# Eight small moves in the written order of a two-block kernel's second block

## The chip, the cores and the metric

The kernel runs on one core of a Trainium2 chip. The metric is the device time of one launch in microseconds (us), the median of three runs. The engines are named as in the profile: PE (TensorE, matmuls and transposes), DVE (VectorE), ACT (ScalarE), POOL (GpSimd), SP (the queue that issues most DMAs).

## The reference, cut to what matters

x is 2 x 1024 tokens of 256 features, all in float32. There are two blocks, each with a residual connection around it.

```
# first block
x = x + soft_moe(attention_with_field(x, cond))      # 16 heads of 16; 64 experts of 32 slots
# second block
h = rotation(x)                                       # a 256 x 256 matrix from quaternions
for l in range(2):                                    # two layers, 8 heads of 64, windows of 128 tokens
    q, k, v = split(shift_token(h) @ wqkv[l])
    q, k = l2norm(q) * q_scale[l], l2norm(k) * k_scale[l]
    q, k = rotary_xpos(q, k)                          # q*cos*scale + rotate_half(q)*sin*scale, k with 1/scale
    h = h + local_attention(q, k, v) @ wo[l]          # each window looks at itself and the one before
    t = shift_token(h)
    t = (t - mean(t)) / sqrt(var(t) + 1e-5) * ln_g[l] + ln_b[l]
    a, g = split(t @ w1[l] + b1[l])                   # 682 + 682 features
    h = h + (a * gelu(g)) @ w2[l] + b2[l]
x = x + h
```

In the soft mixture of experts the output is a product of softmax weights (2048 per token, over all slots) with the experts' outputs. The kernel computes this last product, called the mixing here, partly beside the first windows of the second block.

## The kernel before, in words

**The second block** (from L1060) is one loop over steps s from -2 to 31. There are 32 windows of 128 tokens: window i belongs to layer i // 16, batch i // 8 % 2 and place i % 8. The order of the instructions on PE, DVE, ACT and POOL is the order in which the code issues them; only the order of DMA issues on SP is left to the scheduler. Step s works on several windows at once, in this order:

- project(s+2) (L1115): four matmuls of 128x512 into a PSUM tile pq, for q and k. rotate_parts(s+2) (L1130): ACT copies pq to raw and squares it; DVE multiplies pq with the cosines into t1 (L1143, "the cosine product"); POOL multiplies raw with the sines in two halves into t2 (L1145). Both ACT's copy and DVE's product read the same PSUM banks, and the build orders them one behind the other, as issued.
- scores (L1202): q times k into PSUM. maxima (L1219): four DVE instructions per half of the heads that add the mask, scale and reduce. weights (L1239): four exponentials on ACT per half. turn_e (L1263): transposes of the divided weights of the window before, copied by ACT (first half of the heads) or DVE (second half). mix (L1280): weights times values.
- values and keep_values (L1173): the value projection. turn (L1189): transposes of the rotated q and k. norms(s+2) (L1150): DVE sums the squares (L1154) and makes a first guess z (L1157); POOL refines it in twelve small instructions to zn (L1161 to L1164). rotated(s+2) (L1168): DVE adds t1 and t2 (L1170) and scales the k half with zn (L1171).
- divide (L1254): four divisions per half by the softmax sums, on POOL for the first half, on DVE for the second (L1260).

After every fourth window project_out (L1303) adds the attention's output to the residual into xb (L1314, DVE), and halves (L1324, POOL) adds the two feature halves for the mean of chunks 1 to 6. A chunk is 512 tokens; chunk f runs through forward(s - 7), four steps each: centre(f) makes the mean on PE (L1333), subtracts it on DVE (L1341) and squares on ACT (L1343); normalise(f) makes the variance on PE (L1333), the reciprocal root on ACT by a logarithm and an exponential (L1353, L1354), multiplies on DVE (L1355, hc times rs) and scales on POOL (L1357); gate (L1363) makes one of six pieces of the w1 product; feed (L1394) the w2 product. The first chunk has centre(0) at the end of step 5 and normalise(0) at the end of step 6; its first gates come at the end of step 7.

**The mixing beside it.** In steps -2 to 4, beside(s, point) (L1509) runs one sixteenth of the mixing of the second batch at the points "a", "b" and, in the first two steps, "c" of a step: combine (L902) multiplies a turned piece of the weights with the experts' outputs (at the end of four pieces DVE adds the sum, L920), then turn_w (L883) transposes the next piece (L888) into a two-bank PSUM tile, and ACT (odd pieces, L895) or DVE (even pieces, L897) copies it to xb. READY (L1495) names where the rows of the weights are made: heaviest (the row maximum, DVE), weigh (the exponential, ACT), scale (reciprocal and division by the sum, DVE, L880 and L881). From step 5 on a step is "dense": both halves' scores stand together.

**PSUM.** Two-bank tiles come from two_banks (L1091). There are three: two in the pool ps_b and one in ps_c, called the third. While the mixing runs, the third holds the sums of combine and only the other two rotate. From the first tile behind the last mixing product on, a counter (ring) lets all three rotate, so that each tile takes the place of the one three before it and waits for its readers; the tile with len(ring) % 3 == 1 is the third.

**Tables.** weights2 (L1013) loads the weights of a layer. For "tabs" it issues two DMAs of 512 KB (the cosines and the sines with their scales) and has POOL multiply them with q_scale and k_scale (L1021, four instructions). For the second layer it stands at the end of step 13, behind the second half's divisions.

Of the kernel before, what the change touches and what calls it, by code (L numbers as in the profile page):

```python
# [10 lines left out]
F32 = mybir.dt.float32  # L11
I32 = mybir.dt.int32
AF = mybir.ActivationFunctionType
ALU = mybir.AluOpType
# [3 lines left out]
P = 128  # L18
B = 2
# [11 lines left out]
H1, DH = 8, 64  # L31
# [51 lines left out]
def bcast(ap, axis, n):  # L83

    ap = ap.unsqueeze(axis)
    shape = list(ap.shape)
    shape[axis] = n
    return ap.to_broadcast(shape)
# [3 lines left out]
def tile_kernel(ctx: ExitStack, tc: tile.TileContext, a: dict, out: bass.AP):  # L92
    nc = tc.nc
# [789 lines left out]
    def turn_w(q, jj):  # L883

        pt = wide("pe")
        for j in range(4):
            for i in range(2):
                nc.tensor.transpose(  # L888
                    pt[:, j // 2, (j % 2 * 2 + i) * P : (j % 2 * 2 + i + 1) * P],
                    row(2 * q + i)[:, (4 * jj + j) * P : (4 * jj + j + 1) * P],  # L890
                    ident,
                )
        wTs[q, jj] = xb[:, jj % 2, 1, 1 : 1 + S].rearrange("p (x n) -> p x n", x=2)
        if jj % 2:
            nc.scalar.copy(wTs[q, jj], pt)  # L895
        else:
            nc.vector.tensor_copy(wTs[q, jj], pt)  # L897
        for i in (2 * q + 4, 2 * q + 5):
            if i < T // P:
                fetch(i, jj)  # L900
# [68 lines left out]
    with tc.manual_schedule(  # L969
# [36 lines left out]
        load = {}  # L1006
# [66 lines left out]
    with tc.manual_schedule(  # L1073
# [12 lines left out]
        def third(name):  # L1086
            return ps_c.tile([P, 2, 512], F32, tag="c", name=name)
# [3 lines left out]
        def two_banks(name):  # L1091

            if not mixing:
                ring.append(name)
            return third(name) if len(ring) % 3 == 1 else ps_b.tile([P, 2, 512], F32, tag="b", name=name)

        wide, pair = two_banks, third

# [31 lines left out]
        def rotate_parts(i):  # L1130

            w = i % NWIN
            pq = pqs.pop(i)
            raw = dx0.tile([P, 16, DH], F32, tag="keep", name="raw")
            nc.scalar.copy(raw, pq)  # L1135
            sqs[i] = la.tile([P, 16, DH], F32, tag="t", name="sq", bufs=3)
            nc.scalar.activation(sqs[i], raw, AF.Square)
            t1 = la.tile([P, 16, DH], F32, tag="t", name="t1", bufs=3)
            t2 = la.tile([P, 16, DH], F32, tag="t2", name="t2", bufs=1)
            hf = DH // 2  # L1140
            p4, r4, t14, t24 = (t.rearrange("p (x h) d -> p x h d", x=2) for t in (pq, raw, t1, t2))
            cos, sin = (t[:, :, w, :] for t in load["tabs"])
            nc.vector.tensor_tensor(t14, p4, bcast(cos, 2, H1), ALU.mult)  # L1143
            for lo, hi in ((0, hf), (hf, DH)):
                nc.gpsimd.tensor_tensor(  # L1145
                    t24[:, :, :, lo:hi], r4[:, :, :, hf - lo : DH - lo], bcast(sin[:, :, lo:hi], 2, H1), ALU.mult
                )
            ts[i] = t1, t2
# [167 lines left out]
        def chunk(f):  # L1316

            return f // (B * 2), f // 2 % B, f % 2 * 512
# [28 lines left out]
        def normalise(f):  # L1347
            l, b, t0 = chunk(f)
            hc, sq = hcs[f], hcs.pop((f, "sq"))
            pv = bank("pvar")  # L1350
            sums(f, pv, [sq[:, k, :] for k in range(2)])
            rs = fa["rs"]
            nc.scalar.activation(rs, pv, AF.Ln, bias=eps5)  # L1353
            nc.scalar.activation(rs, rs, AF.Exp, scale=-0.5)  # L1354
            nc.vector.tensor_tensor(hc, hc, bcast(rs, 1, 2), ALU.mult)  # L1355
            for k in range(2):
                nc.gpsimd.tensor_scalar(  # L1357
                    hc[:, k, :], hc[:, k, :], col(f"lg{l}", k), col(f"lb{l}", k), ALU.mult, ALU.add
                )
# [105 lines left out]
        def forward(at):  # L1465

            f, k = divmod(at, 4)
            if at == -2:
                centre(0)
            if at == -1:  # L1470
                normalise(0)
            if not 0 <= f < CHUNKS:
                return
            if k == 0:
                gate(f, 0)
                gate(f, 1)
            if k == 1:
                gate(f, 2)
                gate(f, 3)
            if k == 2:  # L1480
                gate(f, 4)
                if f + 1 < CHUNKS:
                    centre(f + 1)
                gate(f, 5)
            if k == 3:
                if f + 1 < CHUNKS:
                    normalise(f + 1)
                feed(f)


# [7 lines left out]
            (-2, "b"): ((scale, 11),),  # L1498
            (-1, "c"): ((heaviest, 12), (heaviest, 13)),
            (-1, "b"): ((weigh, 12), (weigh, 13)),  # L1500
            (-1, "e"): ((scale, 12), (scale, 13)),
            (0, "c"): ((heaviest, 14),),
            (0, "b"): ((weigh, 14),),
            (1, "c"): ((scale, 14), (heaviest, 15)),
            (1, "b"): ((weigh, 15),),
# [16 lines left out]
        for s in range(-2, WINDOWS):  # L1522
            now, before, nxt, new = (0 <= s + d < WINDOWS for d in (0, -1, 1, 2))

            if new:
                project(s + 2)
                rotate_parts(s + 2)
            ended = 0 <= s - 2 < WINDOWS

            late = s >= WINDOWS - 2
            dense = s > max(PARTS) and not late
            if ended and not dense and not late:
                mix(s - 2, 1)
            if now and dense:
                for hg in range(2):
                    scores(s, hg)
            if ended and dense:
                for hg in range(2):  # L1540
                    if (s - 2, hg) in eTs:
                        mix(s - 2, hg)
            if s == 5:
                rotate(3)
            if now and not dense and not late:
                scores(s, 0)
            beside(s, "a")
            if before:
                turn_e(s - 1, 0)
            if now and not late:  # L1550
                maxima(s, 0)
                weights(s, 0)
            if new:
                values(s + 2)
                keep_values(s + 2)
            beside(s, "c")
            if ended and late:
                for hg in range(2):
                    if (s - 2, hg) in eTs:
                        mix(s - 2, hg)  # L1560
            if now:
                for hg in () if dense else (0, 1) if late else (1,):
                    scores(s, hg)
                for hg in (0, 1) if late else (1,):
                    maxima(s, hg)
                    if hg == 0:
                        weights(s, 0)
            if before and not dense:
                mix(s - 1, 0)
            if nxt:  # L1570
                turn(s + 1)
            if now:
                weights(s, 1)
            if new:
                norms(s + 2)
            beside(s, "b")
            if 0 <= s - 2 < WINDOWS and (s - 2) % 4 == 3:
                project_out((s - 2) // 4)
                if (s - 2) // 4 in halved:
                    halves((s - 2) // 4)  # L1580
            if before:
                turn_e(s - 1, 1)
            if now:
                divide(s, 0)
            if new:
                rotated(s + 2)
            if s == 5:

                f = xp.tile([P, 4 * NS], F32, tag="e", name="f")
                at = 0  # L1590
                for name, k, n in (("u", NF, 512), ("w2", NF, D), ("yo", 2, 512), ("rs", 1, 512), ("sq", 2, 512), ("gl", 2, 512)):
                    fa[name] = f[:, at : at + k * n].rearrange("p (k n) -> p k n", k=k)
                    at += k * n
                fa["rs"] = fa["rs"][:, 0, :]
                fa["hc"] = xin.tile([P, 2, 2, 512], F32, tag="x1", name="hc")
                load["w2"] = fa["w2"]
                load["w1"] = xp.tile([P, NE // 4 * D], F32, tag="y1", name="w1")[:, : 2 * W1N].rearrange(
                    "p (k n) -> p k n", k=2
                )
                weights2(0, "w1", "w2")  # L1600
            forward(s - LAG)
            if now:
                divide(s, 1)
            beside(s, "e")
            if s + 2 == B * NWIN - 1:
                weights2(1, "wqkv", "tabs")
            if s == B * NWIN + 2:
                weights2(1, "wo")
            if s == LAG + 4 * (CHUNKS // 2) - 2:
                weights2(1, "w1")  # L1610
            if s == LAG + 4 * (CHUNKS // 2) - 1:
                weights2(1, "w2")
# [13 lines left out]
        centre(f + 1)  # L1626
        gate(f, 4)
        normalise(f + 1)
        feed(f)
        for n in (0, 1, 2, 3, 5, 4):  # L1630
            gate(f + 1, n)
# [119 lines left out]
```

## Time and profile before

| | |
|---|---|
| median of three runs | 1614.73 us (1613.99 to 1615.87) |
| the profiled execution | 1613.42 us, of it the span 1611.4 us |
| busy, share of the span | PE 98%, DVE 57%, ACT 55%, POOL 33% |
| granted TensorE clock | 1.00 throughout |
| second block (its first projection starts at 846.6): PE busy in 900 to 950, 950 to 1000, 1000 to 1050, 1150 to 1200 | 48.28, 48.69, 47.07, 48.50 of 50 us each |
| PE busy in every other 50 us from 1050 to 1600 | 50.00 of 50 us |
| DVE busy in 1000 to 1050 | 32.77 of 50 us |

A row of the list of waits reads: who waited, "<-" for what, the time in total, how often, the longest. A row of the timeline reads: start and duration in us, engine, line, operation, out<-in, shape, how many were merged; in brackets the idle time before it and what ended that. A matmul in float32 leaves two records. The ends of matmuls are modelled, so that groups on PE overlap by 0.07 or 0.16 us where nothing is waited for.

### The profile page before, as it was taken

How to read it: one execution, taken by the hardware profiler on the slowest of the kernel's cores; microseconds unless marked ns; L12 is line 12 of the kernel's file. 1: busy time of each engine (PE TensorE's matmuls, PEld its weight loads, DVE VectorE, ACT ScalarE, POOL GpSimd, SP SyncE). 2: the span in 40 equal slices, each digit the busy share in tenths (PEclk: the TensorE clock that was granted, in tenths of full speed). 3: DMA queues.
4: the chain of work that ended last, by engine and by line, in shares of the span. 5: the costliest groups of instructions: out<-in, count | busy, mean ns of one | idle time of the engine just before them, and what ended most of it. 6: DMA issues, size and time to landing. Idle time of an engine off the chain costs nothing.

```text
span 1611.4 us, 22677 instructions
## 1 busy us (share of the span) xinstructions
PE 1584.6 (98%) x8672; PEld 805.8 (50%) x8672; DVE 910.6 (57%) x1598; ACT 892.4 (55%) x1662; POOL 538.9 (33%) x830
## 2 busy tenths in 40 slices
PE   8999999999999999999999999999999999999999
PEld 4333333333333444444887666555555555655554
DVE  5768758766773222225455765656576665656532
ACT  2477768777886222226134554666646565666631
POOL 4223323333330100000102345545565555555411
PEclk9999999999999999999999999999999999999999
DMA  5100000010000544455642102000100001000001
GB/s 158 53 14 14 1 15 13 1 21 8 1 1 23 168 142 144 158 166 180 205 123 84 40 1 81 0 1 1 66 1 1 14 1 55 1 1 27 10 18 39
DMA packets 49852, 82.66 MB, mean 51 GB/s; under 512 B 4552, under 2 KB 25200, under 8 KB 49488
## 3 DMA queue, kind: packets, MB, share of 16 engines
q1 hardware_dynamic: 47200, 75.38, 15.4%
q0 software_dynamic: 1584, 5.29, 1.1%
q8 instruction: 68, 1.11, 0.3%
q10 hardware_dynamic: 960, 0.56, 0.1%
q14 instruction: 40, 0.33, 0.1%
HBM read 56.04 MB, written 20.97 MB: 48 GB/s over the span
## 4 chain that ended last, share of the span: by engine, by line
PE 93%; DVE 4%; ACT 1%; issue 1%; DMA 1%; POOL 0%; ACTq 0%; DVEq 0%; POOLq 0%
PE pga L1374 9%; PE sc L329 8%; PE po L347 7%; PE pm L295 7%; PE lg L795 7%; PE sl L821 7%; PE pq L1121 7%; PE cmb L909 5%; PE py L1401 4%; PE pwo L1310 3%; PE po L1290 3%; PE sc L1210 3%; PE pe L1271 3%; PE pv L1177 3%; PE pqk L265 2%; PE py L842 2%
## 5 line engine op out<-in xcount | busy, mean ns | idle before, releaser
L302 DVE TENSOR_REDUCE mx<-pm 128x2 f32<-128x1024 f32 x256 | 302.3, 1219 | 118.1 <-PE pm L295 117.4
L337 ACT ACTIVATE e<-sc 128x512 f32<-128x512 f32 (+1 forms) x500 | 266.1, 612 | 72.3 <-PE pm L295 44.7
L329 PE MATMUL sc<-qs,km 32*128 32x512 f32 x1024 | 254.7, 619 | 0.9 <-DVE qs L317 0.9
L295 PE MATMUL pm<-km,qm 32*128 32x512 f32 x1024 | 246.0, 619 | 2.4 <-ACT xa L432 0.6
L365 POOL TENSOR_TENSOR ob<-ob,part 128x512 f32<-128x512 f32 x101 | 128.3, 1271 | 270.2 <-ACT part L364 270.2
L1374 PE MATMUL pga<-hc,w 128*128 128x512 f32 x320 | 141.8, 593 | 0.0
L1260 POOL TENSOR_SCALAR e<-e,den 128x256 f32<-128x256 f32 (+1 forms) x128 | 130.7, 1034 | 31.4 <-DVE den L1256 31.4
L347 PE MATMUL po<-e,v 128*32 128x512 f32 x1024 | 136.7, 604 | 0.0
L1145 POOL TENSOR_TENSOR t<-raw,tabs 128x512 f32<-128x512 f32 x64 | 81.7, 1296 | 153.6 <-ACT raw L1135 148.3
L329 PEld LDWEIGHTS sc<-qs,km 32*128 32x128 f32 x1024 | 87.6, 183 | 84.5 <-ACT e L337 64.4
L1244 ACT ACTIVATE e<-e,nmx 128x256 f32<-128x256 f32 (+1 forms) x256 | 123.6, 487 | 2.9 <-DVE nmx L1227 2.7
L1121 PE MATMUL pq<-wqo,xa 128*128 128x512 f32 x256 | 115.9, 595 | 1.6 <-DVE xb L897 0.9
L909 PE MATMUL cmb<-xb,y 128*128 128x256 f32 x512 | 116.6, 380 | 0.2 <-ACT xb L895 0.2
L795 PE MATMUL lg<-phi,xa 128*128 128x512 f32 x256 | 115.9, 595 | 0.3 <-ACT xa L432 0.3
L821 PE MATMUL sl<-dsp,xb 128*128 128x512 f32 x256 | 114.9, 592 | 0.0
L295 PEld LDWEIGHTS pm<-km,qm 32*128 32x128 f32 x1024 | 82.8, 183 | 60.0 <-DVE mx L302 31.7
L1227 DVE CUSTOM_DVE_ANT_0 e<-sc,mask,zn 128x256 f32<-128x256 f32 (+1 forms) x256 | 101.9, 460 | 17.4 <-PE sc L1210 17.4
L909 PEld LDWEIGHTS cmb<-xb,y 128*128 128x128 f32 x512 | 94.9, 190 | 16.6 <-issue 3.2
L805 DVE TENSOR_TENSOR l<-lg,keep 128x512 f32<-128x512 f32 x32 | 22.1, 691 | 143.5 <-ACT keep L803 143.5
L1374 PEld LDWEIGHTS pga<-hc,w 128*128 128x128 f32 x320 | 59.0, 190 | 66.6 <-issue 64.5
L1135 ACT COPY raw<-pq 128x1024 f32<-128x1024 f32 x32 | 32.4, 1012 | 107.1 <-PE pq L1121 107.0
L803 ACT COPY keep<-lg 128x512 f32<-128x512 f32 x32 | 18.7, 584 | 125.2 <-issue 107.4
(219 smaller groups left out, 2459.7 us busy)
## 6 DMA issues: line engine op xcount, KB each, us to landing
lgd<-keep SPq DMA_DIRECT2D x64, 256.0 KB, 2.4
w<-in_ffn_W SPq DMA_DIRECT2D x16, 1024.0 KB, 6.9
ebig<-lgd SPq DMA_DIRECT2D x64, 256.0 KB, 3.4
wqo<-in_wqkv SPq DMA_DIRECT2D x2, 1536.0 KB, 7.7
w<-in_w SPq DMA_DIRECT2D x2, 1386.0 KB, 6.1
km<-hk SPq DMA_DIRECT2D x32, 64.0 KB, 2.3
qm<-hq SPq DMA_DIRECT2D x32, 64.0 KB, 2.3
phi<-in_phi SPq DMA_DIRECT2D x1, 2048.0 KB, 7.6
```

Source lines behind the costliest of these rows:

```text
L295: nc.tensor.matmul(pm[:, x, :], qm[u % 2][r, i * P : (i + 1) * P], km[u % 3][r, n * 512 : (n + 1) * 512], start=True, stop=True,)
L302: nc.vector.tensor_reduce(mxs[hu][:, i % 4, 2 * half : 2 * half + 2, n], pm, AX.X, ALU.max)
L329: nc.tensor.matmul(sc[:, x, :] if both else sc[x], km[u % 3][r, j * P : (j + 1) * P], qs[u % 2][r, n * 512 : (n + 1) * 512], start=True, s ...
L337: nc.scalar.activation(part, t, AF.Exp, scale=1.0 / HD0**0.5)
L347: nc.tensor.matmul(po[32 * hh : 32 * hh + 32, :], v[b][:, j, at : at + 32], es[s, hh // 2][:, hh % 2, :], start=True, stop=True,)
L365: nc.gpsimd.tensor_tensor(obs[u, n], obs[u, n], part, ALU.add)
L795: nc.tensor.matmul(lg[:, b, :], xa[:, k, b, 1 + m * P : 1 + (m + 1) * P], phi[:, k, n * 512 : (n + 1) * 512], start=(k == 0), stop=(k == 1),)
L821: nc.tensor.matmul(accs[n][b][:, c, :], xo_tm[:, b * 8 + m, c * P : (c + 1) * P], d[:, b, :], start=(m == 0), stop=(m == 7),)
L909: nc.tensor.matmul(acs[q][:, c, :], y[b][:, 4 * jj + j, c * P : (c + 1) * P], eT[:, j // 2, j % 2 * 256 : (j % 2 + 1) * 256], start=(jj == ...
L1121: nc.tensor.matmul(pq[:, x, :], shifted(xa, k, b, w * WIN, P), load["wqkv"][:, k, x * 512 : (x + 1) * 512], start=(k == 0), stop=(k == 1),)
L1260: engine.tensor_scalar(e[:, x, c, lo:], e[:, x, c, lo:], den[:, x, c : c + 1], None, ALU.mult)
L1374: nc.tensor.matmul(pt[:, x, :], load["w1"][:, k, lo : lo + P], hcs[f][:, k, :], start=(k == 0), stop=(k == 1))
```

## The change

Eight moves, all in the second block or in the mixing beside it; no computation is added or taken away.

- turn_w: for q of 6 and 7 the copies change engines (ACT copies the even pieces, DVE the odd ones).
- two_banks: the third PSUM tile is the third of the rotation (len(ring) % 3 == 0) instead of the first.
- rotate_parts: for window 9 alone DVE's cosine product is issued ahead of ACT's copy of the same tile, so that the copy waits for the product.
- normalise is cut in two: normalise ends with the reciprocal root, normalised has DVE's product and POOL's scaling. For the first chunk normalised(0) stands behind rotate_parts(9) in step 7; for all others both follow each other as before.
- centre(0) moves from the end of step 5 to behind project(8) and rotate_parts(8) in step 6.
- READY: the scale of row 13 moves from point "e" of step -1 to point "c" of step 0.
- In steps 0 to 4 the maxima of the first half stand ahead of point "a" and of the transposes of the window before, instead of behind them.
- The tables of the second layer stand behind norms(15) in step 13, ahead of project_out, the halves and the divisions, and in the code ahead of wqkv. The order of the DMA issues on SP is the same in both kernels (tables, then wqkv).

```diff
         wTs[q, jj] = xb[:, jj % 2, 1, 1 : 1 + S].rearrange("p (x n) -> p x n", x=2)
-        if jj % 2:
+        if jj % 2 != (q > 5):
             nc.scalar.copy(wTs[q, jj], pt)
         else:
             nc.vector.tensor_copy(wTs[q, jj], pt)
...
-            return third(name) if len(ring) % 3 == 1 else ps_b.tile([P, 2, 512], F32, tag="b", name=name)
+            return third(name) if ring and len(ring) % 3 == 0 else ps_b.tile([P, 2, 512], F32, tag="b", name=name)
...
+            sqs[i] = la.tile([P, 16, DH], F32, tag="t", name="sq", bufs=3)
+            t1 = la.tile([P, 16, DH], F32, tag="t", name="t1", bufs=3)
+            cos, sin = (t[:, :, w, :] for t in load["tabs"])
+
+            def cosines():
+                nc.vector.tensor_tensor(
+                    t1.rearrange("p (x h) d -> p x h d", x=2),
+                    pq.rearrange("p (x h) d -> p x h d", x=2),
+                    bcast(cos, 2, H1),
+                    ALU.mult,
+                )
+
+            ahead = i == LAG + 2
+            if ahead:
+                cosines()
             raw = dx0.tile([P, 16, DH], F32, tag="keep", name="raw")
             nc.scalar.copy(raw, pq)
-            sqs[i] = la.tile([P, 16, DH], F32, tag="t", name="sq", bufs=3)
             nc.scalar.activation(sqs[i], raw, AF.Square)
-            t1 = la.tile([P, 16, DH], F32, tag="t", name="t1", bufs=3)
             t2 = la.tile([P, 16, DH], F32, tag="t2", name="t2", bufs=1)
...
-            nc.vector.tensor_tensor(t14, p4, bcast(cos, 2, H1), ALU.mult)
+            if not ahead:
+                cosines()
...
             nc.scalar.activation(rs, pv, AF.Ln, bias=eps5)
             nc.scalar.activation(rs, rs, AF.Exp, scale=-0.5)
+            hcs[f, "rs"] = rs
+
+        def normalised(f):
+            l = chunk(f)[0]
+            hc, rs = hcs[f], hcs.pop((f, "rs"))
             nc.vector.tensor_tensor(hc, hc, bcast(rs, 1, 2), ALU.mult)
...
-            if at == -2:
-                centre(0)
             if at == -1:
                 normalise(0)
...
                 if f + 1 < CHUNKS:
                     normalise(f + 1)
+                    normalised(f + 1)
                 feed(f)
...
-            (-1, "e"): ((scale, 12), (scale, 13)),
-            (0, "c"): ((heaviest, 14),),
+            (-1, "e"): ((scale, 12),),
+            (0, "c"): ((scale, 13), (heaviest, 14)),
...
                 project(s + 2)
                 rotate_parts(s + 2)
+
+            if s == LAG - 1:
+                centre(0)
+            if s == LAG:
+                normalised(0)
...
             if now and not dense and not late:
                 scores(s, 0)
+                maxima(s, 0)
             beside(s, "a")
             if before:
                 turn_e(s - 1, 0)
             if now and not late:
-                maxima(s, 0)
+                if dense:
+                    maxima(s, 0)
                 weights(s, 0)
...
                 norms(s + 2)
+            if s + 2 == B * NWIN - 1:
+                weights2(1, "tabs", "wqkv")
             beside(s, "b")
...
             beside(s, "e")
-            if s + 2 == B * NWIN - 1:
-                weights2(1, "wqkv", "tabs")
```

More of the change, by code (lines that the diff above doesn't have):

```diff
@@ L1133, in rotate_parts @@
             pq = pqs.pop(i)
+            sqs[i] = la.tile([P, 16, DH], F32, tag="t", name="sq", bufs=3)
[11 more added lines that the diff above has]
+                cosines()
             raw = dx0.tile([P, 16, DH], F32, tag="keep", name="raw")
             nc.scalar.copy(raw, pq)
-            sqs[i] = la.tile([P, 16, DH], F32, tag="t", name="sq", bufs=3)
             nc.scalar.activation(sqs[i], raw, AF.Square)
-            t1 = la.tile([P, 16, DH], F32, tag="t", name="t1", bufs=3)
             t2 = la.tile([P, 16, DH], F32, tag="t2", name="t2", bufs=1)
             hf = DH // 2
-            p4, r4, t14, t24 = (t.rearrange("p (x h) d -> p x h d", x=2) for t in (pq, raw, t1, t2))
-            cos, sin = (t[:, :, w, :] for t in load["tabs"])
-            nc.vector.tensor_tensor(t14, p4, bcast(cos, 2, H1), ALU.mult)
+            r4, t24 = (t.rearrange("p (x h) d -> p x h d", x=2) for t in (raw, t2))
+            if not ahead:
+                cosines()
             for lo, hi in ((0, hf), (hf, DH)):
@@ L1628, in tile_kernel @@
         normalise(f + 1)
+        normalised(f + 1)
         feed(f)
```

## The prediction

> **What bounds the kernel now.** I read the page's first two parts first.
>
> ```profile
> span 1611.4 us, 22677 instructions
> ...
> PE 1584.6 (98%) x8672; PEld 805.8 (50%) x8672; DVE 910.6 (57%) x1598; ACT 892.4 (55%) x1662; POOL 538.9 (33%) x830
> ...
> PEclk9999999999999999999999999999999999999999
> ```
>
> TensorE sets the time: 98% busy at the full granted clock, no other engine above 57%. All that reordering can win is its idle time, 26.8 us in all, so next comes the list of PE's own waits.
>
> ```profile
> PE pe L1271 <- DVE t L1143: 4.0, 2, 2.5
> ...
> PE pq L1121 <- DVE xb L897: 0.9, 2, 0.4
> ...
> PE pe L1271 <- DVE xT L920: 0.8, 1, 0.8
> ...
> PE pm L1333 <- DVE xb L1314: 0.4, 1, 0.4
> ...
> PE pe L888 <- DVE t L1143: 0.4, 1, 0.4
> ```
>
> These seven waits (6.6 us of idle) all lie in the second block, and each is at a place that the diff touches. After 1184.97 PE has no wait of 15 ns or more, so what is won before that should reach the end. Third, the timeline around three of them.
>
> ```profile
> 1014.65 1.98 PE L1333 MATMUL pm<-xb,ones_d 128*128 128x512 f32 x4 [0.44 <-DVE xb L1314]
> ...
> 1034.61 0.63 ACT L1354 ACTIVATE f<-f 128x512 f32<-128x512 f32 x1
> ...
> 1035.27 1.30 DVE L1355 TENSOR_TENSOR hc<-hc,f 128x1024 f32<-128x1024 f32 x1 [2.73 <-ACT f L1354]
> ...
> 1036.69 1.89 DVE L1260 TENSOR_SCALAR e<-e,den 128x256 f32<-128x256 f32 x4
> ...
> 1038.50 1.20 DVE L1143 TENSOR_TENSOR t<-pq,tabs 128x1024 f32<-128x1024 f32 x1
> ...
> 1039.85 1.06 PE L1271 MATMUL pe<-ident,e 128*128 128x128 f32 x8 [2.49 <-DVE t L1143]
> ...
> 1179.10 4.69 DVE L1260 TENSOR_SCALAR e<-e,den 128x256 f32<-128x256 f32 x4
> ...
> 1179.80 5.12 POOL L1021 TENSOR_TENSOR tabs<-tabs,rows 128x512 f32<-128x512 f32 x4
> ...
> 1183.71 1.21 DVE L1143 TENSOR_TENSOR t<-pq,tabs 128x1024 f32<-128x1024 f32 x1
> ...
> 1184.97 1.09 PE L1271 MATMUL pe<-ident,e 128*128 128x128 f32 x8 [1.50 <-DVE t L1143]
> ```
>
> The reader is to see two queues of DVE. At 1035 DVE stands for 2.73 us before the chunk's multiplication (L1355), because ACT's reciprocal root is late; four divisions and then the cosine product (L1143) are queued behind it, and PE needs the PSUM tile that this product reads. At 1179 the four divisions take 4.69 us instead of the 1.15 that the same four take at 1153, while POOL multiplies the tables.
>
> **The change, part by part.** Times are on the clock of the trace before; every saving moves what follows. PE starts a group 0.07 or 0.16 us before the modelled end of the group in front, so the end of a wait wins the idle time plus that overlap.
>
> *Scale 13 behind step 0's projection.* One division of a row (L881, 2.29 us at 892.57) leaves the place in front of the cosine product, which would then start when the raw copy ends (892.42) and end at 893.7 instead of 895.99. PE is ready at 895.45: 0.43 + 0.16 = **0.59**. At its new place DVE was idle (3.3 us before 900.40, waiting for a DMA), so it costs nothing; its reader, the transposes at 904, has 6 us to spare. The next PE wait, 0.61 at 914, hangs on POOL's norms (zn at 910.04) and moves along unchanged.
>
> *Copies exchanged, maxima moved ahead of them.* From q = 6 the copy at point "b" goes to ACT, that at "a" to DVE. At "b" of steps 2 and 3 DVE's copy ended at 949.75 and at 971.42, each 0.06 before PE's projection could start. ACT's rows for this copy are 1.01 against DVE's 1.23, ACT is free there (last exponential until 947.09) and its copy can start at 948.53: 0.21 each, **0.42**. The two other "b" copies (904.9, 924.1) had no PE waiting. At "a" DVE's copy would end at 939.72 (transposes end 938.46, plus 1.23) and its first reader of the slot is at 940.98. It must queue behind the maxima, which is why these are issued first: that moves no start, they stand ready at 934.55. Queued behind the copy now: the scale of row 15 (936.17 to about 939.7, needed at 947) and in step 1 that of row 14 and the maximum of row 15, about 0.9 late, with zn then at 926.4 against its use at 929.9.
>
> *Third PSUM tile third.* With three tiles in rotation the phase only matters at the start. The first tile behind the last mixing product took the third buffer and so waited for the sums L920 (991.75); now it takes one whose last readers, the maxima of step 4, ended at 987.2: 0.85 + 0.16 = **1.0**. The third tile, scores of step 5, meets L920 instead, about 3.5 us after it ended. DVE's chain behind (copy 992.93, L1170, L1171, divisions, cosines) starts 1.0 earlier too, as zn (992.33) is ready in time; the projection for the rotation, which started at 999.30 on the heels of these cosines (999.25), moves along.
>
> *First mean behind a projection.* The mean's four matmuls (1.72) no longer stand right behind the sum L1314 (1014.60). PE goes on at 1014.05 with the projection (3.43), then the mean, and the scores start at about 1019.3 instead of 1020.00: **0.70**. On DVE the two subtractions (1.27) go behind the cosines: these come at 1019.6, the subtractions end at 1022.0, and the maxima start at 1021.95 instead of 1022.35. On ACT the square goes behind raw and its square and ends at 1023.1, in time for the copy at 1023.2. The value projection must now wait for the subtractions (PSUM slot): it comes at 1024.05, 2 us later.
>
> *First product behind the cosines.* On the clock shifted by 0.70, the norms' seed z comes at 1026.8 instead of 1027.21 and zn 4.6 after it, as in the trace (1031.81), at about 1031.4; L1171 ends at 1032.1, and the four divisions (1.8) follow at once: 1034.05. The projection ended at 1032.84. Cosines 1034.0 to 1035.2, then raw, which must now wait for them (same banks), to 1036.25. PE reaches its transposes at 1036.6: no wait by a margin of 0.34, **2.49 + 0.07 = 2.56**. The trace has no raw that waits for a product. From one side nothing is lost; from the other, one more collision of POOL's norms with L1170 (an L1161 of 1.24 instead of 0.21) would make all 1.0 later and cost 0.7. I take the margin as worked out; the product of 1.30 then ends at 1036.5, the maxima run from 1036.4 (1039.62 before).
>
> *Tables behind the norms.* Four POOL multiplications (5.12) move from 1179.80 to 1165.74, where POOL stood idle for 4.92 (until 1170.67). The order of SP's queue is not moved: both tables are issued at 1158.74 before the weights, and land after 4.6 (median), about 1164. They end at about 1170.9; the halves' sum (1.09) comes 0.3 later, at 1172.0, PE's mean needs it at 1173.48. The four divisions at 1179.10 then take 1.15, the cosines start with raw's end (1180.70) and PE is not held: 1.50 + 0.07 = **1.57**. POOL's sines also start at 1180.75 instead of 1184.99.
>
> Sum: 0.59 + 0.42 + 1.0 + 0.70 + 2.56 + 1.57 = **6.84 us**. The profiled execution took 1613.42 (span 1611.4 and 2.0 around it), so a profile of the changed kernel would show a span near 1604.6. The median of the three runs is 1.3 above that execution: 1614.73 - 6.84 = **1607.9**.
>
> **Rivals.**
>
> *A. Raw becomes the wait.* The 0.34 margin is a difference of two long chains. For it: DVE is 66% busy in 1000 to 1050, zn is an estimate. Against: PE waits only for what is over the margin. It would leave 0.7, at most 1.5, of the 2.49: 1608.6 to 1609.4.
>
> *B. The first gate waits for the chunk's scaling.* POOL now does the two sines (2.52) before the two scalings (1.76), from raw's end: 1036.29 to 1040.55. The gate comes at 1040.96, its second half at 1041.39: it holds PE only if POOL slips by over 0.84. With both sines as slow as the slowest row (2.26) it would slip by 2.0: 1609.1. In the trace an L1161 of POOL grew from 0.21 to 1.24 beside DVE's L1170 (1029.65). [...]
>
> *C. Another engine takes over the pace.* If DVE's queue, not PE, carried the stretch 890 to 1040, each wait would come back a few instructions on, and only the tables' and half of the cosines' share would last: 1.57 + 1.28, 1611.9, no difference. Against it: every next wait above has a margin.
>
> *D. Slower: POOL's queue stands at the tables.* The multiplications now stand in front of the halves' sum, the divisions and the chunk's square sum, and wait for a DMA. If the second table lands at L, PE's mean is held from L = 1169.8 on (two multiplications 2.56, the halves 1.09). The slowest of the four table loads took 11.1 to land: 1170.6, a wait of 0.8, 1608.7. For a slower kernel PE must lose 10 us, so L at 1180, 20 us after the issue; PE itself would by then wait for the weights behind the tables. Nothing in the trace is near that.
>
> **How the numbers follow.** The forecast 0.62, A 0.14, B 0.06, C 0.12, D as slower 0.03, other places 0.03 slower. What a measurement of this kernel tells from no change is about 0.2%, 3.2 us (the three runs spread over 1.9). Forecast, A and B are faster, 0.82; C is same, 0.12; slower 0.06. Low end: the two PE waits that I leave (0.61 at 914 and 0.66 at 928, for a copy of ACT) could go too with their overlaps, 6.84 + 1.5: 1606.4. High end: A with B, and 1 us for the spread, and part of C: 1611.5. Outside stay most of C, the slower cases and a few in a hundred below.
>
> **What would show it.** Right: in PE's waits the pairs with L897, L920, the first L1314 and both of 2.5 and 1.5 are gone, those with den and xa stay; the product stands behind the cosines; divisions beside POOL's sines at 1.15. Wrong: a PE wait for raw or for POOL's scaling near 1030 to 1036, or for the halves' sum near 1168; PE's idle time unchanged or a new wait after 1180.

## The result, and the profile after

The changed kernel takes 1606.78 us (median of 4 runs, 1606.37 to 1606.99) against 1615.16 us for the kernel before (4 runs, 1613.99 to 1615.87) beside it: a ratio of 0.9952, with a 95% interval of 0.994 to 0.9964. It is faster by 8.4 us, which is more than the 3.2 us that a measurement can tell from no change. In two further comparisons the ratio was 0.9952 (0.9938 to 0.9965; 1606.36 us) and 0.9953 (0.994 to 0.9965; 1607.0 us).

The profiled execution of the changed kernel took 1606.93 us, with a span of 1604.9 (before: 1613.42 and 1611.4). The page's first two parts:

```profile
span 1604.9 us, 22678 instructions
...
PE 1584.1 (99%) x8672; PEld 806.0 (50%) x8672; DVE 905.7 (56%) x1598; ACT 893.0 (56%) x1662; POOL 539.4 (34%) x830
...
PEclk9999999999999999999999999999999999999999
```

PE's busy time is the same within 0.5 us (1584.6 before), so all the gain is idle time of PE. These are PE's waits in the second block, from 840 us to the end; the columns are the total, how often, and the longest:

```profile
PE pe L888 <- DVE ebig L881: 0.8, 1, 0.8
PE pq L1122 <- ACT xa L937: 0.7, 1, 0.7
PE pe L1286 <- DVE nmx L1242: 0.6, 1, 0.6
PE pq L1122 <- ACT xb L896: 0.5, 2, 0.2
PE cmb L910 <- ACT xb L896: 0.2, 1, 0.2
```

What is left is less than 1 us each. The pairs with the cosine product (2.5, 1.5 and 0.4), with the sum L920 and with xb L1314 are gone. The two waits for DVE's copies are halved and now hang on ACT's. PE's idle time from 840 us on (gaps of 15 ns and more) falls from 8.95 to 2.83 us.

The timeline around the first chunk's product, in the changed kernel:

```profile
1030.56 1.68 DVE L1275 TENSOR_SCALAR e<-e,den 128x256 f32<-128x256 f32 x4
...
1032.15 1.21 DVE L1140 TENSOR_TENSOR t<-pq,tabs 128x1024 f32<-128x1024 f32 x1
1032.19 0.63 ACT L1369 ACTIVATE f<-f 128x512 f32<-128x512 f32 x1
...
1033.28 1.26 DVE L1375 TENSOR_TENSOR hc<-hc,f 128x1024 f32<-128x1024 f32 x1
1033.45 1.02 ACT L1152 COPY raw<-pq 128x1024 f32<-128x1024 f32 x1 [0.62 <-DVE t L1140]
...
1034.55 2.52 POOL L1160 TENSOR_TENSOR t<-raw,tabs 128x512 f32<-128x512 f32 x2 [0.64 <-ACT raw L1152]
...
1034.88 1.09 PE L1286 MATMUL pe<-ident,e 128*128 128x128 f32 x8
...
1037.06 1.53 POOL L1377 TENSOR_SCALAR hc<-hc,cols 128x512 f32<-128x512 f32 x2
...
1039.28 3.17 PE L1394 MATMUL pga<-hc,w 128*128 128x512 f32 x7
```

The divisions, the cosine product (L1140), the chunk's product (L1375) stand in this order on DVE without a gap that matters. Raw now waits for the cosines and ends at 1034.47, and PE's transposes start at 1034.88 with no wait. In the kernel before they stood idle for 2.49 us at this place. POOL's scaling ends at 1038.59, and the first gate starts at 1039.28.

The timeline around the second layer's tables, in the changed kernel:

```profile
1163.24 2.50 POOL L1022 TENSOR_TENSOR tabs<-tabs,rows 128x512 f32<-128x512 f32 x2
...
1165.73 1.09 POOL L1341 TENSOR_TENSOR f<-xb 128x512 f32<-128x512 f32 x1
...
1168.54 1.02 PE L1348 MATMUL pm<-f,ones_d 128*128 128x512 f32 x2
...
1174.16 1.55 DVE L1275 TENSOR_SCALAR e<-e,den 128x256 f32<-128x256 f32 x4
...
1175.85 1.23 DVE L1140 TENSOR_TENSOR t<-pq,tabs 128x1024 f32<-128x1024 f32 x1
...
1178.47 1.09 PE L1286 MATMUL pe<-ident,e 128*128 128x128 f32 x8
```

The table multiplications end before the halves' sum (L1341), which ends at 1166.82, 1.7 us before PE's mean. The four divisions take 1.55 us where they took 4.69, and PE's transposes have 1.4 us to spare.

**Where the gain came from.** The table compares the starts of the same groups on PE in the two traces (after minus before), and gives what was gained on the way to each.

| group on PE, its start before | after minus before | gained | the prediction's term |
|---|---|---|---|
| first projection of the second block, 846.62 | +0.52 | | |
| transposes of row 12 and 13, 896.04 | -0.08 | 0.60 | scale 13: 0.59 |
| transposes of the next rows, 912.98 | -0.24 | 0.16 | none |
| projection, 949.81 | -0.44 | 0.20 | copies: 0.21 |
| projection, 971.48 | -0.65 | 0.21 | copies: 0.21 |
| transposes, 991.80 | -1.66 | 1.01 | third tile: 1.0 |
| scores, 1020.00 | -2.41 | 0.75 | first mean: 0.70 |
| transposes, 1039.85 | -4.97 | 2.56 | first product: 2.56 |
| transposes, 1184.97 | -6.51 | 1.54 | tables: 1.57 |

The sum is 7.03 us; the prediction's was 6.84. The first row is not from the change: the time up to there differs by up to 1.4 us between executions of kernels that are the same up to there. Below I therefore use **the rest**, the time from the first projection of the second block to the end of the span. It is 764.81 us before and 757.79 after, 7.02 less; in two more profiles of the changed kernel it is 757.76 and 757.73. The medians differ by 7.2 to 8.4. Where the other part comes from is found with the last experiments.

### The profile page after: what moved, and what is told of

Read it like the earlier page. It is cut to its first block, busy times and chain, and to the rows that moved or that the text cites. A ratio compares the mean times of both kernels' runs of the same rounds, so it can differ in the third digit from the quotient of the medians.

```text
span 1604.9 us, 22678 instructions
## 1 busy us (share of the span) xinstructions
PE 1584.1 (99%) x8672; PEld 806.0 (50%) x8672; DVE 905.7 (56%) x1598; ACT 893.0 (56%) x1662; POOL 539.4 (34%) x830
## 4 chain that ended last, share of the span: by engine, by line
PE 94%; DVE 3%; ACT 1%; DMA 1%; issue 1%; POOL 0%; ACTq 0%; DVEq 0%; POOLq 0%
PE pga L1394 9%; PE sc L329 8%; PE po L347 7%; PE pm L295 7%; PE lg L795 7%; PE pq L1122 7%; PE sl L821 7%; PE cmb L910 6%; PE py L1421 4%; PE po L1305 4%; PE sc L1225 4%; PE pwo L1325 3%; PE pe L1286 3%; PE pv L1192 3%; PE pqk L265 2%; PE py L842 2%
```

## The experiments

Theory: PE alone sets the time of the second block, and each part takes away one wait of PE, so that the parts nearly add up. Rivals: another engine carries the stretch, so that a wait that is undone comes back only in part; or one of the parts is paid for by another.

**Undo one part: the tables back.** The changed kernel with the tables of the second layer at their old place.

```diff
-            if s + 2 == B * NWIN - 1:
-                weights2(1, "tabs", "wqkv")
             beside(s, "b")
...
             beside(s, "e")
+            if s + 2 == B * NWIN - 1:
+                weights2(1, "wqkv", "tabs")
```

> The changed kernel with one move undone: the second layer's tables stand at the end of step 13 again. Theory (each move has its own share, and the shares add): PE's wait of 1.5 us for the cosine product comes back, the four divisions beside the tables take about 4.7 instead of 1.55, the halves' sum comes 0.3 earlier, and the span is 1.55 us above that of the changed kernel, 1606.4. Rival (one early wait is the whole gain, and whatever is late afterwards is caught up): span within 0.4 of the changed kernel's 1604.9.

Measured: 1607.88 us, ratio to the kernel before 0.9965 (0.9952 to 0.9978); the rest is 759.32, 1.53 more than in the changed kernel. The timeline of this run:

```profile
1174.50 4.69 DVE L1275 TENSOR_SCALAR e<-e,den 128x256 f32<-128x256 f32 x4
...
1175.19 5.12 POOL L1022 TENSOR_TENSOR tabs<-tabs,rows 128x512 f32<-128x512 f32 x4
...
1179.11 1.21 DVE L1140 TENSOR_TENSOR t<-pq,tabs 128x1024 f32<-128x1024 f32 x1
...
1180.37 1.09 PE L1286 MATMUL pe<-ident,e 128*128 128x128 f32 x8 [1.50 <-DVE t L1140]
```

The divisions beside POOL's table multiplications are at 4.69 again, to the digit, and PE's wait of 1.50 with them. This part is worth what its wait was worth, with all others in place.

**Undo half a part: raw ahead of the cosines.** The changed kernel, with the chunk's product at its new place but ACT's copy raw issued first for window 9.

```diff
-            ahead = i == LAG + 2
+            ahead = False
```

> The changed kernel, but window 9 too copies raw first and multiplies with the cosines second; the chunk's product still stands behind the cosines. Theory (it is the product's place that counts, not the order of copy and cosines): ACT is free at 1032.82, copies until 1033.85, the cosines run from 1033.9 to 1035.1, and PE, ready at 1034.88, waits about 0.2: span 0.2 to 0.3 above 1604.9. POOL's sines start 0.6 earlier. Rival (issuing the cosines first is what wins the 2.5 us): PE waits 1 us or more, span 1606 or above.

Measured: 1607.80 us, ratio 0.9963 (0.9949 to 0.9977); the rest is 758.99, 1.20 more. That is far more than the 0.2 to 0.3 of the theory, and by its size it is the rival's (1 us or more); by its cause it is neither, as the timeline of this run shows:

```profile
1032.33 0.99 ACT L1152 COPY raw<-pq 128x1024 f32<-128x1024 f32 x1
...
1033.35 1.22 DVE L1140 TENSOR_TENSOR t<-pq,tabs 128x1024 f32<-128x1024 f32 x1 [1.53 <-ACT raw L1152]
1033.47 3.50 POOL L1160 TENSOR_TENSOR t<-raw,tabs 128x512 f32<-128x512 f32 x2
1034.49 1.34 DVE L1375 TENSOR_TENSOR hc<-hc,f 128x1024 f32<-128x1024 f32 x1
...
1034.72 1.06 PE L1286 MATMUL pe<-ident,e 128*128 128x128 f32 x8 [0.18 <-DVE t L1140]
...
1039.13 1.09 PE L1286 MATMUL pe<-ident,e 128*128 128x128 f32 x8 [0.53 <-DVE nmx L1242]
```

The wait that I expected, for the cosines, is there with 0.18. The second, 0.53, I had not listed: behind the cosines on DVE's queue stand the product and the eight maxima of step 7, and all of these are late too. The first maximum starts at 1035.76, against 1034.46 in the changed kernel, although the scores in front of it came 0.41 earlier (1030.64 against 1031.05). PE's second transposes need a tile that the last maximum frees. So the order of cosines and raw is worth 1.2 of the 2.56 us, and only the way through DVE's queue shows it. PE's idle time grew by 0.71; the rest of the 1.20 is overlap between groups on PE that the lateness takes away, 0.17 of it at transposes (1037.51) that stand in no list of waits.

**Undo half a part: the maxima back.** The changed kernel with the copies exchanged, but the maxima of steps 0 to 4 behind the copy at "a", as before.

```diff
             if now and not dense and not late:
                 scores(s, 0)
-                maxima(s, 0)
...
             if now and not late:
-                if dense:
-                    maxima(s, 0)
+                maxima(s, 0)
```

> The changed kernel with the maxima of steps 0 to 4 behind point a again, the copies still exchanged. Theory (DVE's queue is strict, so the maxima now wait behind a copy whose transposes PE has not done): in steps 2, 3 and 4 the maxima start near 939.7 instead of 934.5 and the transposes that need their PSUM tile wait until 941.4, about 3.1 us each; in step 1 about 2.2 more than the 0.61 of now; span 9 to 12 us above 1604.9, slower than the kernel before by 2 to 5. Rival (the maxima were moved for nothing, since other tiles are at hand): within 0.5 of 1604.9.

Measured: 1612.39 us, ratio 0.9989 (0.998 to 0.9999); the rest is 763.37, 5.58 more. The timeline of this run, one of four such places (steps 1 to 4):

```profile
937.79 1.04 PE L888 MATMUL pe<-ident,ebig 128*128 128x128 f32 x8
...
938.86 1.23 DVE L898 COPY xb<-pe 128x1024 f32<-128x1024 f32 x1 [3.86 <-PE pe L888]
940.00 0.47 DVE L1242 CUSTOM_DVE_ANT_0 e<-sc,mask,zn 128x256 f32<-128x256 f32 x1
...
940.23 1.06 PE L1286 MATMUL pe<-ident,e 128*128 128x128 f32 x8 [1.41 <-DVE xb L898]
```

Four waits of 1.41, each for DVE's copy: 5.6 in all, where I expected 3.1 each at three of the places and 2.2 more at the fourth, and a kernel slower than the one before. It is slower than the changed kernel but not than the kernel before, so only half of this came: the maxima, ready since 934, do stand behind a copy that must wait for PE, but the size was wrong. I had PE's transposes of the window before wait for the maxima, whose scores' tile they would take over; but PE started at 940.23, with three of the four maxima still to come, and right behind the copy (940.09). So it waited for the copy alone. Most likely the transposes got the copy's tile in this build; that is read from the wait, not tried by itself. Either way, with all other moves in place the exchange of the copies would have cost 5.6 us without the maxima's move, to win 0.41: moving the maxima is what made it a gain.

**One part alone: the product.** The kernel before, with the chunk's product and scaling behind rotate_parts(9) and the cosines first for window 9, and nothing else of the change.

```diff
+            ahead = i == LAG + 2
+            if ahead:
+                cosines()
             raw = dx0.tile([P, 16, DH], F32, tag="keep", name="raw")
...
+            if s == LAG:
+                normalised(0)
```

> The kernel before with one move alone: for the first chunk the product stands behind the cosines of window 9, which are issued ahead of raw. Theory: the wait of 2.49 goes by itself, since the cosines run from 1034.4 to 1035.6 and raw to 1036.65, before PE's 1037.3: span 2.56 below the kernel before, 1608.9; the waits of 0.85, 0.44 and 1.50 stay. Rival (without the mean's move DVE is too late, so part of the wait stays as a wait for raw): 0.7 to 1.5 less won, 1609.6 to 1610.3.

Measured: 1611.42 us, ratio 0.9982 (0.9973 to 0.9992); the rest is 762.18, 2.63 less than before. PE's waits in this run:

```profile
PE pe L1285 <- DVE t L1139: 1.5, 1, 1.5
...
PE pe L1285 <- DVE xT L920: 0.8, 1, 0.8
```

The wait of 2.49 is gone, the one at the tables and the one for L920 stay. Of the 2.63, 0.10 was gained at 912.98, where none of its edits reaches (more on this below); the other 2.53 are what this part pays among the others.

**Three parts alone: scale 13, third tile, first mean.**

```diff
-            return third(name) if len(ring) % 3 == 1 else ps_b.tile([P, 2, 512], F32, tag="b", name=name)
+            return third(name) if ring and len(ring) % 3 == 0 else ps_b.tile([P, 2, 512], F32, tag="b", name=name)
...
-            if at == -2:
-                centre(0)
...
-            (-1, "e"): ((scale, 12), (scale, 13)),
-            (0, "c"): ((heaviest, 14),),
+            (-1, "e"): ((scale, 12),),
+            (0, "c"): ((scale, 13), (heaviest, 14)),
...
+            if s == LAG - 1:
+                centre(0)
```

> The kernel before with three of the moves alone: the scale of row 13, the third PSUM tile, the first mean. Theory: each takes away its own wait and nothing else, 0.59 at 895, 1.0 at 991 and 0.70 at 1014, 2.3 us together; the waits of 0.44 twice, 2.49 and 1.50 stay as they are. The changed kernel won 0.16 more at 912, where PE's transposes started 0.07 after the end of the cosines of window 3: if this comes from the copies' exchange, as DVE then has one copy less in step 0, it is not here; if it comes from the scale, it is. Rival (the waits hand on to each other): the 2.49 grows by what is won in front of it, and less than 1 us is left.

Measured: 1611.74 us, ratio 0.9986 (0.9977 to 0.9995); the rest is 761.96, 2.85 less than before. The waits at 895, 991 and 1014 are gone. The three moves were not tried one by one; what each is worth is read from its place in the table above. The wait for the cosines near 1037 did not grow:

```profile
1035.60 1.67 POOL L1357 TENSOR_SCALAR hc<-hc,cols 128x512 f32<-128x512 f32 x2
...
1036.56 1.21 DVE L1143 TENSOR_TENSOR t<-pq,tabs 128x1024 f32<-128x1024 f32 x1
...
1037.91 1.06 PE L1271 MATMUL pe<-ident,e 128*128 128x128 f32 x8 [2.22 <-DVE t L1143]
```

It is 2.22 instead of 2.49, since the chain behind it (the chunk's root on ACT, the product, the divisions, the cosines) moved up a little more than PE did. That 0.27 is part of the 2.56 in the table above, so the shares of the parts overlap by as much. Without the overlap the parts add up: 2.85 + 2.63 + 1.53 + 0.41 (the copies, from the table) - 0.27 = 7.15, against 7.02 for all of them. The 0.10 at 912.98 stands in both the 2.85 and the 2.63; counted once, the sum is 7.05.

**Beyond the change: halves of a copy on two engines.** The changed kernel, with the copies that PE still waits for (pieces 0 and 2 of the last rows, and rotate(2)) cut in halves, one on ACT and one on DVE.

```diff
-        if jj % 2 != (q > 5):
+        if q > 6 and jj % 2 == 0:
+            nc.scalar.copy(wTs[q, jj][:, 0], pt[:, 0])
+            nc.vector.tensor_copy(wTs[q, jj][:, 1], pt[:, 1])
+        elif jj % 2 != (q > 5):
...
-        nc.scalar.copy(xa[:, :, b, 1 + n * 512 : 1 + (n + 1) * 512], pt)
+        if h == 2:
+            nc.scalar.copy(xa[:, 0, b, at], pt[:, 0, :])
+            nc.vector.tensor_copy(xa[:, 1, b, at], pt[:, 1, :])
```

> The changed kernel, with three copies of a two-bank tile halved, ACT taking the first bank and DVE the second: the turned pieces (7, 0) and (7, 2) and the rotated tile of the third half. Theory (PE's waits of 0.23, 0.23 and 0.66 are the length of one copy of 1.01 behind the transposes, so half as long a copy takes them away): the first two go, the third falls to about 0.2, PE's idle time is about 0.9 less and the span 0.9 to 1.0 shorter; in runs without a profile this is within the spread. Rival (two engines on neighbouring banks get in each other's way, or DVE's own next copy comes late): no gain or a loss at turn_e's copies behind.

Measured: 1607.89 us, ratio 0.9959 (0.9946 to 0.9971), beside 1606.36 for the changed kernel on the same chip; the rest is 758.64, 0.88 more. The timeline of this run:

```profile
948.70 0.59 ACT L896 COPY xb<-pe 128x512 f32<-128x512 f32 x1 [1.35 <-PE pe L888]
949.32 0.69 DVE L897 COPY xb<-pe 128x512 f32<-128x512 f32 x1 [0.74 <-ACT xb L896]
...
950.07 2.41 PE L1130 MATMUL pq<-wqo,xa 128*128 128x512 f32 x5 [0.53 <-DVE xb L897]
```

My expectation fell. DVE's half does not run beside ACT's: its idle time ends with ACT's half. The two readers of one PSUM tile stand one behind the other, as raw and the cosine product do, and 0.59 + 0.69 is longer than the 1.01 of the whole copy. PE's waits of 0.23 became 0.53 each, and the one of 0.67 became 0.96.

**The changed kernel again,** beside the last two.

> The changed kernel once more, on the chip of the next one, for the comparison: span 1604.5 to 1605.5, PE waits as before.

Measured: 1606.36 us (1606.07 to 1606.88), the rest 757.76 and PE's idle time 2.83, both as in the first profile.

**What the medians hold beside the waits.** By then the medians differed by more (7.9 and 8.4 us) than the rest does (7.0). In the lists of runs, 10 of 36 executions of the kernel before and 5 of 10 with the three moves had a mean granted clock of 0.999 instead of 1.000 and were about 1 us longer; no other kernel had one. Both have a PE wait of over 2 us in the second block (2.49 and 2.22). (In eight traces, among them those of the kernel before and of the changed kernel, PE also waits 6.2 to 6.5 us for its first weights. In these two the first matmuls behind that wait start 0.85 us apart (the first two 0.98) and later ones of the same line 0.43, so they too ran at half the rate; the trace's clock record begins only there, at 10.5 and 11.4 us, and the views print 1.00 ahead of it. That is alike in both kernels and lies outside the stretch compared.) Two kernels put such a wait into the changed kernel, one at its old place, one far from it, and the changed kernel ran beside them.

The first has the product and scaling back in step 6, and raw first:

```diff
             if at == -1:
                 normalise(0)
+                normalised(0)
...
-            ahead = i == LAG + 2
+            ahead = False
...
-            if s == LAG:
-                normalised(0)
```

> The changed kernel with the first chunk's product and scaling back at the end of step 6 and raw ahead of the cosines again; all else as changed. It puts the long wait of PE for the cosines near 1035 back. Theory (the parts are near to additive): that wait is 2.2, as in the run with three moves, the stretch from the second block's first projection to the end takes 757.8 + 2.3 = 760.1, the median is about 1609. Second theory: executions at a granted clock of 0.999, about 1 us longer, were seen in 10 of 36 runs of the kernel before and 5 of 10 with three moves, in none of 44 of the others; what these two kernels have alone is a PE wait over 2 us in the second block. By it some of these runs show 0.999 again. Rival (it is the chip or chance): none does.

The second issues the cosine product of window 22 four times:

```diff
             if not ahead:
-                cosines()
+                for _ in range(4 if i == 22 else 1):
+                    cosines()
```

> The changed kernel with the cosine product of window 22 (step 20, far behind every place of the change) issued four times instead of once, three of them work for nothing. The products are 1.21 each, so 3.63 more on DVE; with the margin of about 1.4 that the same product has in step 14 (cosines end 1177.08, PE starts 1178.47) PE waits about 2.2 and the stretch grows by 2.2 to 2.4, to about 760.1; median about 1609. If a PE wait over 2 us is what brings the granted clock of 0.999, some runs show it here too, and are about 1 us longer; if the place near 1035 or the kernel before's order is what brings it, none does.

And the changed kernel:

> The changed kernel itself, on the same chip as the two runs beside it: 1606.4 to 1606.8, the stretch 757.8, the granted clock 1.000 in every run if a PE wait over 2 us is what brings 0.999.

Measured: 1609.61 us (ratio 0.9973, 0.9963 to 0.9983) with the product back, 1610.7 us (0.9979, 0.997 to 0.9988) with the wait elsewhere, 1607.0 us for the changed kernel. The granted clock was 0.999 in 4 of 8 runs of the first (median 1610.33, against 1609.38 of the other four), in 10 of 11 of the second, in none of 5 of the changed kernel. The profiles of the two fell on such runs. The first one's timeline, and then its granted clock in short stretches (the columns are the stretch, its length, PE's busy time with the instructions, the granted clock, and the DMA share and rate):

```profile
1036.18 1.67 PE L1286 MATMUL pe<-ident,e 128*128 128x128 f32 x8 [2.22 <-DVE t L1140]
...
1037.64 3.00 PE L1192 MATMUL pv<-wqo,xa 128*128 128x512 f32 x4
```

```profile
1034.00:1035.00 1.00, 0.00 (x0) 1.00 0.00 0
1035.00:1036.00 1.00, 0.00 (x0) 1.00 0.00 0
1036.00:1037.00 1.00, 0.82 (x5) 0.74 0.00 0
1037.00:1038.00 1.00, 1.00 (x5) 0.50 0.00 0
1038.00:1039.00 1.00, 1.00 (x2) 0.50 0.00 0
1039.00:1040.00 1.00, 1.00 (x2) 0.55 0.00 0
1040.00:1041.00 1.00, 1.00 (x7) 1.00 0.00 0
```

Behind the wait PE's clock is granted at half for about 3.4 us (worked out from the four stretches below 1: 0.26 + 0.50 + 0.50 + 0.45 of a us lost, 1.7, at half speed). The value projection takes 3.00 where it takes 1.88 in the profile before. The rest is 761.7 in this run, 3.9 more than in the changed kernel: 2.29 for the wait with its overlap and 1.7 for the clock; without the latter it is 760.0, where 760.1 was expected. With the wait of 2.46 near 1302 the granted clock is 0.50 from 1304 to 1307, and the rest is 762.1.

So in these two traces a wait of 2.2 to 2.5 us cost 1.7 us on top of itself, at two places far from each other. Between the medians of the executions at 0.999 and at 1.000 it is less, 0.9 to 1.3 us in three kernels, and the single execution at 1.000 of the run with the wait elsewhere was not shorter than the others; why is not shown. Over all runs whose clock is listed, the kernels with such a wait in the second block show 0.999 in 35 of 83 executions (16 of 54 of the kernel before, 5 of 10, 4 of 8, 10 of 11), those without in none of 49. Among these are the kernels whose longest wait in this part is 1.50.

## Why the prediction was right, point by point

The time lay in the range, on the faster side as forecast, 1.1 us below the predicted 1607.9. No rival occurred.

- *Scale 13 behind step 0's projection*: 0.60 at its own place against 0.59. Of the 0.16 more up to 912.98, 0.06 is of this move too: right behind 896 the second transpose is 0.06 further ahead in every run with the move, and not in the run with the product alone. The other 0.10 is gained at 912.98 itself and is not shown to be of any move. The product-only run, which has none of the moves up to there, gained the same 0.10, and the run with the wait elsewhere, which is the changed kernel up to there, lost 0.04. The maximum of a row (L868, at 900.40 in the trace before) waits there for its DMA, and PE starts these transposes 12.58 us behind it there and 12.66 in the changed kernel, so the 0.10 may come from when the DMA lands in an execution; that is an estimate, no run shows it. PE's start hung on the cosines (they ended at 912.93, PE started at 912.98) without idle time, because the wait is shorter than the overlap; so it stands in no list. The 0.61 at 914 stayed, as said, but its releaser is now the maxima.
- *Copies exchanged*: 0.41 against 0.42. That it is a gain at all rests on the maxima, as the run with the maxima back shows.
- *Third PSUM tile third*: 1.01 against 1.0.
- *First mean behind a projection*: 0.75 against 0.70.
- *First product behind the cosines*: 2.56 against 2.56, the step that I was least sure of. The margin between raw's end and PE is 0.41 against 0.34, and raw waits for the cosines as argued. Without the cosines first, 1.20 of it would be lost. Rival A (raw becomes the wait) was thus close, and did not come.
- *Tables behind the norms*: 1.54 against 1.57. The divisions take 1.55 and not 1.15, so this one sign of being right did not come; the 1.4 us to spare in front of PE hide the difference. Rival D would have shown at the halves' sum, which ends 1.7 us ahead of PE's mean.
- Rival B: the scaling ends 0.69 ahead of the gate. POOL's first sine starts at 1034.55, 0.08 behind raw's end (1034.47) and just as DVE's product ends (1034.54); the trace gives raw as what ended POOL's idle time. With raw first the sines (1033.47 to 1036.97) overlap with the cosines and the product on DVE (to 1035.83), and the two sines take 3.50 instead of 2.52; why they take longer there is not shown.
- Rival C: the waits that were put back one at a time returned at their full size (the tables at 1.50, the product at 2.22, as in the run with three moves), and the parts taken alone add up. PE carries the stretch.

The term that was off most is none of the six. It is the last step, "the median of the three runs is 1.3 above that execution: 1614.73 - 6.84". I took what the median has above the profiled execution as fixed. Against the profiled execution itself the sum gives 1613.42 - 6.84 = 1606.6, and the profiled execution after took 1606.93; its first projection started 0.52 later, and the rest was 0.18 shorter than the sum says. Where the clock of every run is listed, the runs of the kernel before at a clock of 1.000 have medians of 1613.8 to 1614.0, and those at 0.999 of 1614.7 to 1615.0; so a part of what the median has above the profiled execution is most likely the executions at 0.999, 0.9 to 1.1 us longer, and of the changed kernel's 14 executions none was at 0.999. For the three runs of the prediction the clock is listed only for the profiled one, so that some of them were at 0.999 is likely and not shown. The trace could not have told: in that execution the clock was 1.00 behind the 2.49 wait.

## What to carry to other kernels

Where one engine is 98% busy, list its own waits, price each as its idle time plus the overlap of the groups around it, and follow every in-order queue behind a moved instruction to its next reader: six terms worked out in this way came within 0.05 us each at their own places. Look for two things that the list does not show: waits shorter than the overlap, and instructions further back in the same queue (the maxima, in two of the runs here). Two TensorE waits here, of 2.22 and 2.46 us, cost 1.7 us more than their length in the traced executions, so look at the granted clock of every execution, not of the profiled one alone.

## What the runs showed of the hardware that was not expected

- **The clock behind a wait.** After 2.22 us without work (the product back) and 2.46 us (the wait elsewhere) TensorE's granted clock was 0.50 for about 3.4 us in the traces. Not every such wait shows it: behind the 2.49 of the kernel before and the 2.22 of the three moves the clock in the trace was 1.00. Over the executions, a mean clock of 0.999 came in 16 of 54 of the kernel before, 5 of 10 with the three moves, 4 of 8 with the product back and 10 of 11 with the wait elsewhere, and in none of 15 of the two kernels whose longest wait in the second block is 1.50. Why it comes in some executions and not in others, and so much more often in one kernel, is not shown.
- **Two readers of one PSUM tile.** ACT's and DVE's halves of one copy ran one behind the other (0.59, then 0.69), though they read different halves of the tile. DVE's idle time ended with ACT's half, so it was held until then. The halves also go into one tile in SBUF. The run does not tell whether the order comes from the shared PSUM tile or from that, nor whether the chip would have let them overlap.
- **The start of the kernel.** The first projection of the second block starts anywhere from 846.2 to 847.5 us, in kernels that are the same up to there. Half a microsecond between two spans therefore says nothing about the second block.
